# Turning the last hop's results in 32x32 blocks on VectorE instead of TensorE, with some other moves

## The chip, the cores and the metric

The kernel runs on one core of a Trainium2 chip. A core has five engines that run side by side, each with its own instruction queue: TensorE (PE, matrix products and transposes into PSUM), VectorE (DVE), ScalarE (ACT), GpSimd (POOL) and SyncE (SP). In this kernel SP's queue issues most loads, POOL's queue issues the stores and the loads of features and also computes a small power, and ScalarE's queue loads the weights. Arrays that are written out and read again lie in the chip's main memory; the working tiles lie in SBUF. The metric is the device time of one execution in microseconds (us), as the median of several runs.

## The reference

The input is a matrix of features x (2708 x 512) and a weighted, symmetrically filled adjacency adj (2708 x 2708), both in float32. Four graph layers follow one another, each as x = layernorm(x + layer(x)):

```python
def _layernorm(x, axis=-1, eps=1e-5):
    m = jnp.mean(x, axis=axis, keepdims=True)
    v = jnp.var(x, axis=axis, keepdims=True)
    return (x - m) / jnp.sqrt(v + eps)

# layer 0: mean over neighbours, with a normalised mask added to the matrix
mask = adj > 0
head = mask / max(sqrt(sum(mask * mask, -1)), 1e-12)
inc = adj + head
layer0 = (inc @ x) / sum(inc, -1)

# layer 1: attention over the graph and a plain graph product, both gated
h = x @ W_sa
scores = s_left[:, None] + s_right[None, :]          # from h and a_sa
e = where(adj != 0, exp(-leaky_relu(scores, 0.01)), 0)
x_a = (e / (sum(e, 1) + 1e-5)) @ h
x_b = adj @ (x @ W_gcnb) + b_gcnb
layer1 = sigmoid(attn_a * x_a + attn_b * x_b)        # attn_*: sigmoid gates from adj @ x and x

# layer 2: four weights, three hops
out = x @ weight[0]; p = x
for idx in range(1, 4):
    p = adj @ p
    out = out + p @ weight[idx]

# layer 3: degree-normalised product, then a dense layer
a_hat = adj + eye
dinv = rsqrt(deg)                                    # deg = max(count of adj != 0 in a row, 1)
pooled = (dinv * a_hat * dinv) @ x + x
layer3 = relu(pooled @ W + b)
```

## The kernel before

**Products.** Every product with the adjacency is done in blocks of Strassen's kind: the matrix is cut in halves (1354 rows each) and the seven products of sums of blocks are formed; in layers 2 and 3 this is done at two levels, 7 x 7 products. VectorE forms the sums of adjacency blocks (tiles called z, s, t, a), TensorE multiplies them (accumulators accu, accc, accd, acca), and VectorE and ScalarE add the results into tiles called q. Layer 2 is evaluated from the inside: the stage before the hops forms Y0 = x W3, and each of the three hops multiplies with the adjacency and adds one more term x W. Results of a sweep are transposed: features lie on partitions and nodes along the row. So a result has to be turned before it can be normed by row or be loaded as the next product's operand.

**Order of the work.** A Python function builds a list of events: `at(pos, fn)` notes that `fn` emits its instructions at position `pos`. The list is sorted by position and run, so positions are the kernel's own clock. One unit is some 12 to 13 us. The stages start at `S[s] = 28 * s`: S[0] is layer 0, S[1] and S[2] are layer 1 (S[2] ends with layer 2's first products), S[3], S[4] and S[5] are the three hops, S[6] is layer 3. A tile scheduler then orders each engine's instructions. `held` events and the early part of the list are kept in the list's order by extra dependencies without a semaphore (the loop at the end of the kernel, L1758 to 1767).

**A hop.** `sweep2` (L1351) runs over two ranges of columns, g = 0 and 1 (338 and 339 columns, times two blocks). In each range the 49 products end with two half ranges h of the nodes, and for each of these a function done(p0, dp, g, i0, n, h, cc, tiles) is called with six tiles: four of 128 nodes and two of 82 or 83. The adjacency loads of the whole sweep are issued on SP's queue, in the list's order (`load`, L1373).

**What follows a hop.** After the first two hops it is `hop_done` (L1551 to 1575): for each tile, VectorE does four block transposes (L1565; each 32x32 block is turned by itself, and the blocks are laid out by the output's access pattern) into a row buffer y, and POOL's queue stores it with four DMAs (L1570), whose rows come out in the right order in memory. After the last hop it is `done5` (L1577 to 1587): TensorE turns the tile with four transposes into a PSUM bank ps_n (`untranspose2`, L1541, instructions at L1544); `layernorm` (L598) forms the statistics on VectorE (bn_stats L600, bn_aggr L602, add L604), a power on POOL (L605), one more small operation on VectorE (L607) and the scaling on ScalarE (L610); `store2` (L1321) stores the rows to X3 on POOL's queue (L150 and L152). Row buffers come from one set of six (`nat`), used in turn.

**The next layer's operand.** `next_x2(S[6], X3)` (L308) loads X3 as the quarters B11, B12 (into T3), B21, B22 on POOL's queue, and VectorE forms their sums. `next_x(S[1], ...)` does the same for layer 1's sweep, out of X1, which layer 0 stores with POOL.

**Other places that the change touches.** `extra1` counts the nonzero entries of the adjacency in masks (tally, L1042), for the degrees, on VectorE. `prep2` (L1157) forms the attention weights e on ScalarE (L1163, L1164) and masks them on VectorE (L1165). `pairs2` (L1224) works off two half ranges of layer 1 together: it norms, turns (f), forms sums (z, L1193) and multiplies with W3 (g, L692). `ext_loads` and `ext_sums` (L1331, L1340) load blocks of layer 2's transposed input and store their sums Es for the hops. `done6` (L1639) does the dense layer, the norm and the output of layer 3.

The function done5 and its caller are the core:

Of the kernel before, what the change touches and what calls it, by code (L numbers as in the profile page):

```python
# [21 lines left out]
F32 = mybir.dt.float32  # L22
BF = mybir.dt.bfloat16
AF = mybir.ActivationFunctionType
# [3 lines left out]
NH = 1354  # L28
# [40 lines left out]
def gnn_kernel(ctx: ExitStack, tc: tile.TileContext, x, adjT, w_sa, a_sa, w_gcn, b_gcn, wab, bab, w_hop, w_out,  # L69
               b_out, out):  # L70
    nc = tc.nc
# [52 lines left out]
        return [dram.tile([wt(t % KT), D], F32, name=f"{nm}{t}", tag=f"{nm}{t}") for t in range(NT)]  # L124

    X1, XB, X2, Y0, X3 = (feature(nm) for nm in ("X1_", "XB_", "X2_", "Y0_", "X3_"))
    Y1, Y2 = ([dram.tile([NH, D], F32, name=f"{nm}{h}", tag=f"{nm}{h}") for h in range(2)] for nm in ("Y1_", "Y2_"))
    X0 = [x[h * NH + k * P : h * NH + k * P + wt(k), :] for h in range(2) for k in range(KT)]
    OUT = [out[h * NH + k * P : h * NH + k * P + wt(k), :] for h in range(2) for k in range(KT)]

# [45 lines left out]
    events = []  # L176

    held = set()

    def at(pos, fn, hold=False):  # L180

# [68 lines left out]
    def x_load(src, k, s, eng):  # L250
# [2 lines left out]
        t = b12_tile(k) if s == "B12" else new_x(s, k)  # L253
        move(eng, t[:w], q)

    def next_x(base, src, sums=0.95, halves=-0.25):


        q = nc.gpsimd

        ql = nc.scalar if base == S[1] else q
        at(base + 1.3, lambda: rest_x(src, ql))
        for k in range(KW):
            f = k / KT
            if (k * P) < RANGES[-1][0]:
                at(base - 5.8 + f, lambda k=k: x_load(src, k, "B11", q))
                at(base - 1.85 + f, lambda k=k: x_load(src, k, "B22", q))
                at(base - 1.84 + f, lambda k=k: x_load(src, k, "B12", q))
                at(base + (0.03 if base == S[1] else -1.15) + f, lambda k=k: x_sums(k), True)
                at(base - 0.85 + f, lambda k=k: x_load(src, k, "B21", q))  # L270
                at(base + 1.5 + f, lambda k=k: x_last(k), True)
            else:
                at(base + halves + 0.05 * (k - 8), lambda k=k: x_load(src, k, "B22", ql))
                at(base + max(halves, 0.1) + 0.05 * (k - 8), lambda k=k: x_load(src, k, "B21", ql))
                at(base + sums + 0.03 * (k - 8), lambda k=k: x_sums(k), True)
                at(base + 2.6 + 0.03 * (k - 8), lambda k=k: x_last(k), True)
# [31 lines left out]
    def next_x2(base, src, ext_src=None, one=False, plus=False, swapped=False):  # L308
# [7 lines left out]

        def go(s, ks, ext):
            for k in ks:
                x_load(src, k, s, q)
            if ext and ext_src is not None:  # L320
                c0 = HD if s in ("B12", "B22") else 0
                for i, g in enumerate("BD"):
                    r0 = (HD if s in ("B21", "B22") else 0) + i * P
                    h = "T3" if s == "B12" else s
                    if g == "D" and ks[-1] < 8:
                        group(h, g)
                    t, w = groups[h, g][0][:, 2, :], ext_src[r0 : r0 + P, :]
# [13 lines left out]
        if plus:  # L341
            at(base - 1.4, lambda: residual("B22"), True)
            at(base + 1.9, lambda: residual("B11"), True)
        for s, p in (("B22", 0.0 if one else -1.95), ("B21", 0.02), ("B11", late), ("B12", late + 0.15)):
            ks = list(range(KW))
            if s in early:
                lo, m = early[s]
                at(base + lo, lambda s=s, m=m: go(s, range(m), True))
                ks = range(m, KW)
            at(base + p, lambda s=s, ks=ks: go(s, ks, ks[0] == 0))  # L350
# [244 lines left out]
                     [(h * KT + k, k * P - R0, wt(k)) for k in ts])  # L595


    def layernorm(dsts, y, w, on_scalar=False, late=None):  # L598
        st = small.tile([P, 6], F32, name="st")
        nc.vector.bn_stats(st[:w], y[:w])  # L600
        mv = small.tile([P, 2], F32, name="mv")
        nc.vector.bn_aggr(mv[:w], st[:w])  # L602
        rstd = small.tile([P, 2], F32, name="rstd")
        nc.vector.tensor_scalar(rstd[:w, 0:1], mv[:w, 1:2], EPS, None, ALU.add)  # L604
        nc.gpsimd.tensor_tensor(rstd[:w, 1:2], rstd[:w, 0:1], neg_half[:w], ALU.pow)  # L605
        if on_scalar:
            nc.vector.scalar_tensor_tensor(rstd[:w, 0:1], mv[:w, 0:1], -1.0, rstd[:w, 1:2], ALU.mult, ALU.mult)  # L607
        for d, c0, c1 in dsts:
            if on_scalar:
                fn = lambda d=d, c0=c0, c1=c1: nc.scalar.activation(d[:w], y[:w, c0:c1], AF.Identity,  # L610
                                                                    bias=rstd[:w, 0:1], scale=rstd[:w, 1:2])
                fn() if late is None else late.append(fn)
                continue
            nc.vector.tensor_scalar(d[:w], y[:w, c0:c1], mv[:w, 0:1], rstd[:w, 1:2], ALU.subtract, ALU.mult)
# [416 lines left out]
    def extra1(pb, r, R0, n, A):  # L1031
# [9 lines left out]
                d = deg[R0, h]  # L1041
                nc.vector.scalar_tensor_tensor(d[:w, :n], a[:w, :n], 0.0, d[:w, :n], ALU.not_equal, ALU.add)  # L1042

        for ij, p in (("11", -0.6), ("21", 0.05), ("22", 1.05), ("12", 3.6)):
            for k in range(KW):
                at(pb + p + 0.8 * k / KT, lambda ij=ij, k=k: tally(int(ij[0]) - 1, (ij, k)), r == 0)
        for h, p in ((1, 2.0), (0, 4.5)):
# [151 lines left out]
    def pairs2(p0, R0, n, C, tiles):  # L1199
        Y = {}  # L1200
        at(p0 + 0.2, lambda: Y.update(row_sums({(i, c): C[1 - i, c] for i in range(2) for c in range(DC)}, n)))
        for i, (t0, lo, w) in enumerate(tiles):
# [45 lines left out]
            for j in range(2):  # L1248
                at(p + 0.26 * j, lambda j=j, b=b: b(j))
                at(p + 0.45 + 0.02 * j, lambda j=j, e=e: e(j))  # L1250
                at(p + 0.84 + 0.06 * j, lambda j=j, f=f: f(j), nc.tensor)
                at(p + 1.22 + 0.22 * j, lambda j=j, g=g: g(j), nc.tensor)
            at(p + 0.4, c)
            at(p + 0.92, z)

    def done2(p0, dp, last, R0, n, h, C, tiles):
        if not last:
# [288 lines left out]


    for i in range(4):
        for g, p in enumerate((S[2] + 19.3 + 1.1 * i, S[3] + 6.6 + 1.3 * i)):
            a = ({}, g, i // 2, i % 2)  # L1550
            at(p, lambda a=a: ext_loads(*a))  # L1551
            at(p + 0.5 + 0.6 * g, lambda a=a: ext_sums(*a))
# [22 lines left out]
        return done  # L1575

    def done5(p0, dp, g, i0, n, h, cc, tiles):  # L1577
        for i, (s, lo, w) in enumerate(tiles):
            r0 = i0 + s * n + lo

            def b(s=s, lo=lo, w=w, r0=r0):
                ps = untranspose2(cc, s, lo, w)
                y = nat("o")
                layernorm([(y, 0, D)], ps, w, True)
                store2(X3, y, h, r0, w)

            at(p0 + 0.1 + 0.24 * i, b)
# [51 lines left out]
    def done6(p0, dp, g, i0, n, h, cc, tiles):  # L1639

        end = (g, h) == (1, 0)
        def finish(s, lo, w, x, y):

            nc.vector.scalar_tensor_tensor(x[:w], y[:w], 0.0, x[:w], ALU.max, ALU.add)
            layernorm([(x, 0, D)], x, w, True)
            r0 = i0 + s * n + lo
            move(nc.sync, out[h * NH + r0 : h * NH + r0 + w, :], x[:w])
# [77 lines left out]
    for n, i in enumerate(list(nc.cur_bb.bb.instructions)):  # L1725
# [5 lines left out]
        if n < strict:  # L1731
            last[i.engine] = i
        done[i.engine] = i


# [35 lines left out]
```

## Time and profile before

| what | value |
|---|---|
| median of 3 runs | 2843.93 us (2843.19 to 2844.54) |
| profiled execution | 2845.44 us |
| its span | 2843.7 us |
| PE busy | 2802.4 us, 11550 instructions |
| DVE busy | 2247.7 us, 5862 instructions |
| ACT busy | 533.7 us, 1124 instructions |
| POOL busy | 617.2 us, 1114 instructions |
| HBM read and written | 425.35 MB and 83.66 MB, 179 GB/s over the span |

The span is the profiler's time from the first to the last instruction; the profiled execution's own time lies 1.74 us above it. Busy times are sums over an engine's instructions, and matrix products that overlap are counted once in an engine's share. POOL's busy time includes the issue of its DMAs; SP's DMA issues do not count as busy. In a line for a group of instructions the fields are: line, engine, operation, output and inputs, shapes, count, then busy time, mean ns of one, and the idle time of the engine just before them with what released it. In a timeline the first two numbers are start and duration in us, and brackets hold the idle time before.

### The profile page before, as it was taken

The page shows a single profiled execution, that of the slowest core. Times are in us where ns is not written, and L with a number is a line of the kernel's source. Part 1 is how long each engine was busy: PE and PEld are TensorE (multiplying, and loading weights), DVE is VectorE, ACT ScalarE, POOL GpSimd, SP SyncE. Part 2 cuts the span into 40 slices and gives each one's busy share as a digit, 9 for nine tenths or more (in the row PEclk, how much of TensorE's full clock was granted, in tenths as well). Part 3 has the DMA queues.
Part 4 walks back from the last instruction along what each step waited for, and adds up shares of the span by engine and source line. Part 5 has one row for each costly group of instructions (what it writes and reads, how often), then busy time and mean ns, then how long its engine had stood idle before and what let it go on. Part 6 is the DMA issues. An engine that isn't in the chain of part 4 may idle for free.

```text
span 2843.7 us, 38764 instructions
## 1 busy us (share of the span) xinstructions
PE 2802.4 (99%) x11550; PEld 1939.7 (68%) x11550; DVE 2247.7 (79%) x5862; ACT 533.7 (19%) x1124; POOL 617.2 (22%) x1114
## 2 busy tenths in 40 slices
PE   7999999999999999999999999999999999999998
PEld 6899765658755667866666666666666666666665
DVE  6999699668737676775699778897888878899987
ACT  4644100101155353450100000000000100100001
POOL 0223223214310011223113033030330211601202
PEclk9999999999999999999999999999999999999999
DMA  8765476446534242665678667566675666854542
GB/s 234 241 195 184 140 228 218 150 131 196 189 92 139 78 152 69 203 194 158 205 205 255 192 208 234 163 210 203 197 235 173 189 194 180 243 167 146 179 142 90
DMA packets 370291, 511.72 MB, mean 180 GB/s; under 512 B 63632, under 2 KB 323460, under 8 KB 370080
## 3 DMA queue, kind: packets, MB, share of 16 engines
q1 hardware_dynamic: 303544, 371.61, 44.1%
q0 software_dynamic: 49376, 126.39, 13.3%
q10 hardware_dynamic: 17160, 11.24, 1.4%
q8 instruction: 92, 1.51, 0.2%
q14 instruction: 119, 0.97, 0.1%
HBM read 425.35 MB, written 83.66 MB: 179 GB/s over the span
## 4 chain that ended last, share of the span: by engine, by line
PE 86%; DVE 7%; issue 2%; DMA 1%; SPq 1%; ACT 1%; POOL 1%; POOLq 0%; DVEq 0%; ACTq 0%
PE accu L1437 12%; PE accd L1437 12%; PE accc L1437 12%; PE accu L489 7%; PE accd L489 7%; PE acca L1437 6%; PE ps L692 5%; PE accc L489 5%; PE acca L489 4%; PE accr L1508 2%; PE ps_d L653 2%; PE accd L475 2%; PE accc L475 2%; PE accu L475 2%; PE acca L475 1%
## 5 line engine op out<-in xcount | busy, mean ns | idle before, releaser
L1382 DVE TENSOR_TENSOR z<-z 128x339 f32<-128x339 f32 (+1 forms) x966 | 456.8, 507 | 10.9 <-PE accu L1437 2.9
L605 POOL TENSOR_TENSOR rstd<-rstd,neg_half 128x1 f32<-128x1 f32 (+3 forms) x91 | 61.2, 674 | 770.5 <-DVE rstd L604 484.0
L1455 ACT COPY q<-accu 128x338 f32<-128x338 f32 (+1 forms) x84 | 34.6, 443 | 996.5 <-PE accu L1437 836.2
L1437 PE MATMUL accc<-s,t 128*128 128x338 f32 (+1 forms) x644 | 198.1, 450 | 0.0
L1437 PE MATMUL accd<-z,t 128*128 128x338 f32 (+1 forms) x644 | 193.9, 448 | 1.4 <-DVE q L1519 1.4
L1437 PE MATMUL accc<-z,t 128*128 128x338 f32 (+1 forms) x644 | 193.5, 448 | 0.5 <-ACT q L1455 0.5
L1437 PE MATMUL accu<-z,t 128*128 128x338 f32 (+1 forms) x644 | 193.8, 448 | 0.0
L1570 POOL DMA_DIRECT2D Y<-y x192 | 104.8, 552 | 362.8 <-DVE y L1565 331.3
L419 DVE TENSOR_TENSOR a<-a,a 128x384 f32<-128x384 f32 (+2 forms) x330 | 164.2, 514 | 6.7 <-PE accu L489 5.5
L1437 PEld LDWEIGHTS accc<-s,t 128*128 128x128 f32 x644 | 120.9, 190 | 64.1 <-issue 7.5
L1437 PEld LDWEIGHTS accc<-z,t 128*128 128x128 f32 x644 | 122.0, 190 | 61.6 <-issue 1.0
L1437 PEld LDWEIGHTS accd<-z,t 128*128 128x128 f32 x644 | 121.9, 190 | 61.1 <-DVE q L1519 2.1
L1437 PEld LDWEIGHTS accu<-z,t 128*128 128x128 f32 x644 | 121.8, 190 | 59.9 <-issue 0.5
L1382 DVE TENSOR_TENSOR s<-z 128x338 f32<-128x338 f32 (+1 forms) x322 | 150.6, 506 | 9.1 <-PE accc L1437 7.7
L1461 DVE TENSOR_TENSOR q<-q,accd 128x338 f32<-128x338 f32 (+1 forms) x112 | 56.3, 503 | 122.4 <-PE accd L1437 122.4
L1163 ACT ACTIVATE e<-row,s_right 128x384 f32<-128x384 f32 (+5 forms) x176 | 95.7, 570 | 119.8 <-PE accc L489 28.5
L1165 DVE SCALAR_TENSOR_TENSOR a<-a,e 128x384 f32<-128x384 f32 (+2 forms) x160 | 77.0, 507 | 35.7 <-ACT e L1164 25.1
L1042 DVE SCALAR_TENSOR_TENSOR masks<-a,masks 128x384 bf16<-128x384 f32 (+2 forms) x152 | 76.0, 507 | 12.3 <-DMA a<-in_adjT 11.3
L422 POOL DMA_DIRECT2D As<-a x120 | 64.7, 542 | 88.3 <-DVE a L419 64.0
L829 DVE SCALAR_TENSOR_TENSOR s<-a,row 128x384 f32<-128x384 f32 (+2 forms) x152 | 75.8, 511 | 7.5 <-ACT row L814 7.5
L825 DVE TENSOR_TENSOR run<-run,a 128x384 f32<-128x384 f32 (+2 forms) x156 | 77.9, 499 | 1.4
L1164 ACT ACTIVATE e<-e 128x384 f32<-128x384 f32 (+5 forms) x176 | 78.7, 477 | 1.4
(787 smaller groups left out, 5957.6 us busy)
## 6 DMA issues: line engine op xcount, KB each, us to landing
z<-As SPq DMA_DIRECT2D x320, 169.5 KB
z<-As SPq DMA_DIRECT2D x320, 169.0 KB
a<-in_adjT SPq DMA_DIRECT2D x240, 192.0 KB
z<-in_adjT SPq DMA_DIRECT2D x240, 169.5 KB
z<-in_adjT SPq DMA_DIRECT2D x240, 169.0 KB
a<-in_adjT SPq DMA_DIRECT2D x120, 165.0 KB
a<-in_adjT SPq DMA_DIRECT2D x112, 128.0 KB
As<-a POOLq DMA_DIRECT2D x60, 192.0 KB, 3.5
```

The source lines that it names most:

```text
L419: nc.vector.tensor_tensor(A[r, dst, k][:, :n], A[r, a, k][:, :n], A[r, b, k][:, :n], op)
L475: nc.tensor.matmul(B[home, c][:, c0 : c0 + w], a[:, i * P : (i + 1) * P], x[:, d : d + w], start=bool(start and c0 == 0), stop=stop, skip_ ...
L489: nc.tensor.matmul(B[home, c][:, :n], X[STAT[p], k][:, c * P : (c + 1) * P], A[r, MOV[p], k][:, :n], start=bool(start and k == k0), stop=k ...
L692: nc.tensor.matmul(H[home][:w], Y[a, c][:, lo : lo + w], wop(v, c), start=part == 0 and home in "ud" and c == 0, stop=c == 1, skip_group_c ...
L825: nc.vector.tensor_tensor(run[R0, h][:w, :n], run[R0, h][:w, :n], t[:w, :n], ALU.add)
L1042: nc.vector.scalar_tensor_tensor(d[:w, :n], a[:w, :n], 0.0, d[:w, :n], ALU.not_equal, ALU.add)
L1163: nc.scalar.activation(e[:w, :n], row[R0, h][:w, :n], AF.Prelu, bias=s_right[:w, t : t + 1], alpha=0.01)
L1164: nc.scalar.activation(e[:w, :n], e[:w, :n], AF.Exp, scale=-1.0)
L1165: nc.vector.scalar_tensor_tensor(a[:w, :n], a[:w, :n], 0.0, e[:w, :n], ALU.not_equal, ALU.mult)
L1382: nc.vector.tensor_tensor(d[:, :n], Z[x + (k,)][:, :n], Z[y + (k,)][:, :n], op)
L1437: nc.tensor.matmul(B[home][:, :n], stat(v, k), a[:, :n], start=bool(start and k == 0), stop=k == nk - 1, skip_group_check=True)
L1570: nc.gpsimd.dma_start(out=rows[:, :, f * P : (f + 1) * P], in_=o[32 * f : 32 * (f + 1), : m * P].rearrange("p (b d) -> p b d", d=P))
```

## The change

The last hop's results are turned as those of the first two hops are, except in the half range (g, h) = (1, 0), which is the last. For the other three half ranges VectorE turns blocks, POOL stores the tile to a new array Y3, SP's queue fetches it as rows, and the layernorm works on that tile. The rows come with their blocks in a different order along the row, so ScalarE's scaling writes with a permuted access pattern (`swapped`). X3 is stored as before.

Several positions in the list move too: some loads of features get a dependency without a semaphore on the last power emitted before them (`behind_power`, `powers`, `ties`), which orders them behind it on POOL; layer 1's late B11 loads come 0.5 units later, and layer 3's B22 loads 0.65 later; the first range's count masks of block 11 come 0.75 later; in pairs2 the turning, the sums and the products come 0.04 to 0.07 later; the sums Es for the first range of the hops come 1.2 to 2.25 units earlier; and the first half range of layer 3 is worked off 0.35 units later.

```diff
-    Y1, Y2 = (...)
+    Y1, Y2, Y3 = (...)
+    powers, ties = [], []
+    def behind_power(fn):
+        n = len(nc.cur_bb.bb.instructions)
+        fn()
+        if powers:
+            ties.extend((i, powers[-1]) for i in range(n, len(nc.cur_bb.bb.instructions)))
...
-                at(base - 5.8 + f, lambda k=k: x_load(src, k, "B11", q))
-                at(base - 1.85 + f, lambda k=k: x_load(src, k, "B22", q))
-                at(base - 1.84 + f, lambda k=k: x_load(src, k, "B12", q))
+                for s, p in (("B11", 5.8 - 0.5 * (base == S[1] and k > 2)), ("B22", 1.85), ("B12", 1.84)):
+                    at(base - p + f, lambda k=k, s=s: behind_power(lambda: x_load(src, k, s, q)))
...
-                x_load(src, k, s, q)
+                behind_power(lambda: x_load(src, k, s, q)) if base == S[6] else x_load(src, k, s, q)
...
-        for s, p in (("B22", 0.0 if one else -1.95), ("B21", 0.02), ("B11", late), ("B12", late + 0.15)):
+        for s, p in (("B22", 0.0 if one else -1.3 if base == S[6] else -1.95), ("B21", 0.02), ("B11", late), ("B12", late + 0.15)):
...
-    def layernorm(dsts, y, w, on_scalar=False, late=None):
+    def swapped(t):
+        return t.rearrange("p (c f d) -> p f c d", c=4, d=32)
+    def layernorm(dsts, y, w, on_scalar=False, late=None, swap=False):
...
+        powers.append(len(nc.cur_bb.bb.instructions) - 1)
...
+                o, i = d[:w], y[:w, c0:c1]
+                if swap:
+                    o, i = swapped(o), i.rearrange("p (f c d) -> p f c d", c=4, d=32)
+                fn = lambda o=o, i=i: nc.scalar.activation(o, i, AF.Identity, bias=rstd[:w, 0:1], scale=rstd[:w, 1:2])
...
-        for ij, p in (("11", -0.6), ("21", 0.05), ("22", 1.05), ("12", 3.6)):
+        for ij, p in (("11", -0.6 if r else 0.15), ("21", 0.05), ("22", 1.05), ("12", 3.6)):
...
-                at(p + 0.84 + 0.06 * j, lambda j=j, f=f: f(j), nc.tensor)
-                at(p + 1.22 + 0.22 * j, lambda j=j, g=g: g(j), nc.tensor)
+                at(p + 0.9 + 0.06 * j, lambda j=j, f=f: f(j), nc.tensor)
+                at(p + 1.26 + 0.22 * j, lambda j=j, g=g: g(j), nc.tensor)
-            at(p + 0.92, z)
+            at(p + 0.99, z)
...
-        for g, p in enumerate((S[2] + 19.3 + 1.1 * i, S[3] + 6.6 + 1.3 * i)):
+        for g, p in enumerate((S[2] + 18.1 + 0.75 * i, S[3] + 6.6 + 1.3 * i)):
...
     def done5(p0, dp, g, i0, n, h, cc, tiles):
+        if (g, h) != (1, 0):
+            hop_done(Y3)(p0, 0.24, g, i0, n, h, cc, tiles)
+            for i, (s, lo, w) in enumerate(tiles):
+                got = {}
+                r0 = i0 + s * n + lo
+                def a(w=w, r0=r0, got=got):
+                    got["y"] = y = nat("ld")
+                    move(nc.sync, y[:w], Y3[h][r0 : r0 + w, :])
+                def b(w=w, r0=r0, got=got):
+                    o = nat("o")
+                    layernorm([(o, 0, D)], got["y"], w, True, swap=True)
+                    store2(X3, o, h, r0, w)
+                at(p0 + 0.75 + 0.24 * i, a)
+                at(p0 + 1.05 + 0.24 * i, b)
+            return
...
     def done6(p0, dp, g, i0, n, h, cc, tiles):
+        if (g, h) == (0, 0):
+            p0 += 0.35
...
+    instructions = list(nc.cur_bb.bb.instructions)
+    for i, j in ties:
+        tc.add_manual_dep(instructions[i], instructions[j].name,
+                          mybir.DependencyInfo(mybir.DependencyClass.NoSync, mybir.DependencyReason.DATA),
+                          reason="order of the list")
```

More of the change, by code (lines that the diff above doesn't have):

```diff
@@ L126, in gnn_kernel @@
     X1, XB, X2, Y0, X3 = (feature(nm) for nm in ("X1_", "XB_", "X2_", "Y0_", "X3_"))
-    Y1, Y2 = ([dram.tile([NH, D], F32, name=f"{nm}{h}", tag=f"{nm}{h}") for h in range(2)] for nm in ("Y1_", "Y2_"))
+    Y1, Y2, Y3 = ([dram.tile([NH, D], F32, name=f"{nm}{h}", tag=f"{nm}{h}") for h in range(2)] for nm in ("Y1_", "Y2_", "Y3_"))
     X0 = [x[h * NH + k * P : h * NH + k * P + wt(k), :] for h in range(2) for k in range(KT)]
@@ L609, in layernorm @@
             if on_scalar:
-                fn = lambda d=d, c0=c0, c1=c1: nc.scalar.activation(d[:w], y[:w, c0:c1], AF.Identity,
-                                                                    bias=rstd[:w, 0:1], scale=rstd[:w, 1:2])
+                o, i = d[:w], y[:w, c0:c1]
+                if swap:
+                    o, i = swapped(o), i.rearrange("p (f c d) -> p f c d", c=4, d=32)
+                fn = lambda o=o, i=i: nc.scalar.activation(o, i, AF.Identity, bias=rstd[:w, 0:1], scale=rstd[:w, 1:2])
                 fn() if late is None else late.append(fn)
```

## The prediction

> **What bounds the kernel.** I read the busy shares first, then TensorE's share slice by slice, its waits, the windows in which the changed work lies, and the chain of waits at two places.
>
> ```profile
> PE 2802.4 (99%) x11550; PEld 1939.7 (68%) x11550; DVE 2247.7 (79%) x5862; ACT 533.7 (19%) x1124; POOL 617.2 (22%) x1114
> ...
> PE   7999999999999999999999999999999999999998
> ...
> DVE  6999699668737676775699778897888878899987
> ```
>
> TensorE is busy 2802.4 of 2843.7 us; the granted clock is 1.00 in every window below. So an instruction taken off TensorE is time won, unless another engine comes too late with the next operand. VectorE is second, at 79%, but above 90% in single stretches. TensorE's waits, longest sums (which tile waits for which, total, times, longest):
>
> ```profile
> PE ps L692 <- DVE d L1193: 4.4, 3, 3.4
> PE accd L489 <- DVE a L419: 3.3, 3, 1.5
> PE accd L1437 <- DVE q L1519: 1.4, 1, 1.4
> ```
>
> Behind the first 100 us these and a few shorter ones are all the idle time there is, some 15 us. Windows of 50 us, the first in the hop before, the others in the last hop (PE, PEld, DVE, ACT, POOL busy, then clock, DMA):
>
> ```profile
> 1850.00:1900.00 50.00, 50.00 (x182) 33.00 (x181) 45.92 (x112) 1.67 (x4) 9.64 (x18) 1.00 0.66 197
> 2200.00:2250.00 50.00, 50.00 (x201) 32.94 (x200) 46.81 (x117) 6.31 (x10) 13.07 (x22) 1.00 0.61 181
> 2250.00:2300.00 50.00, 50.00 (x192) 33.86 (x191) 39.95 (x102) 6.31 (x10) 15.35 (x27) 1.00 0.67 203
> 2400.00:2450.00 50.00, 50.00 (x194) 33.45 (x193) 35.65 (x93) 4.66 (x6) 25.80 (x46) 1.00 0.83 245
> ```
>
> In the last three lie the 18 tiles whose transposes move (six each near 2211-2231, 2265-2281, 2397-2417). TensorE never rests there.
>
> **The sum** is made against the profiled execution: 2845.44 us (span 2843.7), 1.51 above the median of 2843.93.
>
> *1. TensorE transposes, -7.9.* Each tile has four, between products:
>
> ```profile
> 2211.07 0.60 PE L1544 MATMUL ps_n<-ident,q 128*128 128x128 f32 x4
> 2211.50 0.73 PE L1437 MATMUL accu<-z,T3B 128*128 128x338 f32 x2
> ```
>
> From the start of the four to the start of the next product is 0.43 us; over all 24 tiles it adds up to 10.49, 0.437 each. 18 tiles: 7.9 us. The other end is the group's busy time, 14.4 us for 96, so 10.8 for 72; busy times overlap their neighbours', so I take the former. These lie on the path, since the windows are full. The Trainium skill ("VectorE: DVE Perf Modes", Rules for kernel authors) speaks against the move: for 128x128 it says to use TensorE where the result may lie in PSUM, and gives 390 ns on TensorE against 311 on VectorE (for blocks of 32 only, and in bf16). By its figure the 72 would return an estimated 28 us; the trace's own 0.437 for four decides.
>
> *2. VectorE in the last hop, +1 (0 to +6).* The same block transposes already run behind the earlier hops:
>
> ```profile
> L1565 DVE STREAM_TRANSPOSE y<-q 128x128 f32<-128x128 f32 x128 | 30.2, 286 | 0.1
> L1565 DVE STREAM_TRANSPOSE y<-q 128x96 f32<-128x96 f32 x64 | 12.4, 246 | 0.0
> ```
>
> 12 tiles x 4 x 0.286 + 6 x 4 x 0.246 = 19.6 us, 6.5 for each half range. The statistics cost the same (0.69 from PSUM or SBUF). In the first window 46.8 + 6.5 is 3.3 over 50; but the norms (some 1 us a tile) move about 12 us later, and TensorE runs 4 to 5.5 us behind VectorE there, with a least gap of 2.0. The other windows have 10 and 14 us free. The window of the hop before, with transposes of this kind, stands at 45.9 of 50 and TensorE does not wait. So 0 to 3.3 for the first, with 1 taken, and up to 6 if a second half range is caught too. ScalarE's norm with a permuted output is in no row; from SBUF a norm takes 0.81 and ScalarE is busy 6 of 50, so even doubled it only delays the store.
>
> *3. Round trip through memory, 0 (0 to +8).* POOL gets 72 more stores at 0.552 each, 40 us, all beside other work at 13 to 26 busy of 50. They land in 3.7 us. SP gets 24 fetches of 0.33 to 0.45. A fetch waits for its tile's store and for a buffer (a tile now takes three of the six shared row buffers, not one); I work out that it comes 7 to 10 us after the transposes, against 1.1 + 2.2 + 3.7 = 7.0 for transposes, four issues and landing. So it may hold SP for 4 to 6 us, and the adjacency loads behind it; those are issued 20 to 30 us before TensorE uses them and 10 to 16 before VectorE does, so they are covered. X3 then comes later, and the first loads of the next layer behind it:
>
> ```profile
> 2424.39 0.51 POOL L152 DMA_DIRECT2D X<-o  x1
> 2424.89 1.64 POOL L150 DMA_DIRECT2D B22C<-X  x3
> 2426.53 0.54 POOL L150 DMA_DIRECT2D B22D<-X  x1
> 2427.38 0.54 POOL L150 DMA_DIRECT2D B22D<-X  x1 [0.32 <-DVE z L1382]
> ```
>
> VectorE needs that B22 at 2450.2 (difference t), TensorE 1 us later. I put the last X3 store at 2430 and the last B22 at 2437, 12 us early. If all my spare is an error, the first product waits as much as X3 is later still: 8 taken as the end.
>
> *4. POOL's order at the end of layer 0, -3.3 (-3.3 to 0).*
>
> ```profile
> 345.84 0.54 POOL L150 DMA_DIRECT2D B11B<-X  x1 [4.54 <-DMA X<-o]
> 346.39 0.56 POOL L605 TENSOR_TENSOR rstd<-rstd,neg_half 128x1 f32<-128x1 f32 x1
> ```
>
> A load of B11 stands on POOL's queue ahead of the power and waits 4.54 us for the X store to land (the chain has that store for 5.67 from 339.65). VectorE waits for that power until 346.99, its sums come late, and TensorE waits 0.69, 1.10 and 1.48 at 348 to 357: 3.27. The ties put these loads behind all the powers listed before them, so the chain is cut. What is next late: the loads of T3B and T3C (B12), which move from 347-355 to about 400, and ten count masks of 0.5 that move to about 430, with VectorE at 47.9 and 46.4 of 50 and TensorE less than 1 us behind it. Price 0 to +3, 0.5 taken.
>
> *5. Layer 1 to 2, -4 (-7.2 to +2).* TensorE rests 7.2 us between 971 and 1257, 3.36 of it at 1234 before a product on sums of VectorE:
>
> ```profile
> 1222.94 0.22 issue
> 1223.16 0.01 POOLq L1345
> 1223.17 5.70 DMA Es<-s
> 1228.87 0.02 issue
> 1228.89 0.58 ACT e L1163
> 1229.47 0.02 issue
> 1229.49 0.49 ACT e L1164
> ```
>
> ScalarE's e waits for a ring buffer that an Es store holds, issued behind other POOL work. The Es sums move from 1176-1254 to about 1170-1192, so this wait goes (3.36), and POOL is lighter at 1256 (0.85). Turning and products 0.04 to 0.07 units later (0.5 to 0.9 us) give or take under 1. Against it: more ring buffers and 4 sums at a time at 1160-1190, where VectorE has 37.8 of 50: up to +2. -4 is the two waits.
>
> *6. First range of layer 3 later by 0.35 units (some 4.5 us), -1 (-2.7 to +2).* TensorE waits 1.35, 0.80 and 0.54 there (2574 to 2598); some goes, some is only moved.
>
> Sum: -7.9 + 1 + 0 - 3.3 + 0.5 - 4 - 1 = -14.7. 2845.4 - 14.7 = 2830.7; less 1.5, 2829.2 for a median, rounded to 2830.
>
> **Rivals.**
> - *Only the transposes count.* Waits 4 to 6 are replaced by others as long (VectorE is thin in all three places). -7.9 + 1 = -6.9: 2837 (2834 to 2841). For it: a wait removed often uncovers the next. Against: 4 and 5 each have one named releaser, a DMA landing, that leaves the chain.
> - *VectorE becomes the bound in the last hop.* The three windows do not absorb the 19.6 us; each half range stalls by its own 3.3, 10 in all, and part of 4 and 5 fails (4): -14.7 - 1 + 10 + 4 = -1.7, so 2842, no change. For: 46.81 of 50. Against: 39.95 and 35.65 in the others.
> - *Slower: SP is held.* A fetch that waits on SP beyond 10 us starves VectorE's z, and TensorE with it; the fetch needs POOL's stores, which stand behind powers and X3 stores of earlier tiles, so tiles can hold each other up. It is slower than before when the 18 fetches exceed the cover by over 14.7 us together, 0.8 each; at 1.5 each it is +27 - 14.7 = +12, 2856. For: all six row buffers in turn, and a queue that issues loads in 8 of the 20 us from 2225. Against: POOL is busy 26 to 50% there, and SP's own work has gaps of 3 to 5 us between groups of loads.
> - *The change does not do what it says:* TensorE would not gain if it waited after each transpose anyhow. The full windows exclude it.
>
> **The numbers.** Chances: my forecast 0.58 (own range 2821 to 2836), only the transposes 0.22, VectorE bound 0.10, SP held 0.10. The measurement tells 0.2% (5.7 us) from no change: the bounds are 2838.2 and 2849.6. Faster: all of the first, 0.20 of the second: 0.78. Same: the rest of the second and the third, with 0.02 of the fourth: 0.14. Slower: 0.08. The low end takes the best bounds, though not all together: -10.8 - 3.3 - 7.2 - 2.7 = -24 gives 2820; I take 2821. The high end, 2843, takes in the second rival and the third, and leaves out the fourth.
>
> **What would show it.** Right: 24 transposes on line 1544's successor, not 96; TensorE's busy time down by about 10.8; 264 block transposes on VectorE; TensorE still at 50 of 50 in the three windows, which come some 6 to 8 us earlier; no waits at 348-357 and at 1234. Wrong: new TensorE waits on z or s of line 1382's successor behind SP (the third rival or the second: VectorE idle for a DMA in the one, at 50 of 50 in the other); a wait for t at the start of layer 3 (step 3); TensorE's waits at 400-450 for T1 or for a (step 4); or the sum of idle time as before, though the named waits are gone.

## The result and the profile after

The changed kernel takes 2851.72 us (median of 9 runs, 2850.40 to 2853.32), the kernel before 2843.77 beside it (9 runs): a ratio of 1.0028 with a 95% interval of 1.0019 to 1.0037. It is slower by 8 us where 14 less were forecast. The profiled execution took 2852.80 us with a span of 2851.0, 7.36 more than the span before.

The shares of the page, changed kernel:

```profile
PE 2797.6 (98%) x11478; PEld 1932.3 (68%) x11478; DVE 2258.7 (79%) x5934; ACT 532.2 (19%) x1122; POOL 660.2 (23%) x1186
```

72 transposes are gone from TensorE, 72 block transposes came to VectorE and 72 stores to POOL. TensorE's busy time fell by 4.8 us (from 2802.4), and not by the 10.8 named as a sign. The windows of the last hop (PE, PEld, DVE, ACT, POOL busy, clock, DMA):

```profile
2200.00:2250.00 50.00, 47.42 (x171) 29.99 (x170) 43.95 (x117) 5.62 (x9) 21.24 (x38) 0.97 0.72 224
2250.00:2300.00 50.00, 49.11 (x171) 31.87 (x169) 43.71 (x125) 5.74 (x9) 26.24 (x46) 1.00 0.74 221
2400.00:2450.00 50.00, 50.00 (x186) 32.25 (x185) 40.41 (x116) 4.89 (x6) 35.55 (x66) 1.00 0.89 278
```

TensorE now rests in the first two, and the clock granted in the first is 0.97. VectorE, where I had feared 53 of 50, is at 43.95: it has time left, and yet TensorE waits for it. TensorE's waits behind the first 100 us, longest sums:

```profile
PE ps L706 <- DVE ld L715: 4.9, 3, 3.3
PE accu L496 <- DVE B11D L628: 3.3, 1, 3.3
PE ps_t L656 <- DVE ld L628: 2.5, 2, 1.7
PE accd L1451 <- DVE z L1396: 2.1, 4, 1.0
PE accu L1451 <- DVE z L1396: 1.9, 2, 1.1
PE accc L1451 <- DVE s L1396: 1.6, 1, 1.6
```

The waits of layer 0's end and of 1234 that stood in the list before are gone (accd for a has 0.8 left, ps for d 0.8), and others stand in their place.

**Where the time went.** I match the same products in the two traces, in order, and subtract their start times. The difference is flat where nothing happens and steps where a kernel gains or loses, so it says which stretch paid. For the changed kernel against before, one profiled execution each (us of the kernel before; stretches left out are flat):

| stretch | step | what it is |
|---|---|---|
| 0 to 330 | -1.0 | not the change: it is there by 90 us, before any edit acts, and other kernels here stand between -2.4 and +1.0 |
| 330 to 365 | -3.0 | end of layer 0 |
| 365 to 470 | +6.6 | a wait of 3.26 near 428, and half the clock behind it |
| 470 to 1300 | -0.8 | layers 1 and 2 |
| 2200 to 2430 | +1.4 | last hop: -7.9 for the transposes, +9.2 for waits and half clock |
| 2480 to 2830 | -1.6 | layer 3 |
| 2830 to the end | +5.9 | work ends 1.5 later, the span 7.4 later |

Three losses of 6 to 9 us, then, against three gains that came nearly as forecast (transposes, end of layer 0, layer 3) and one, in layers 1 and 2, that hardly came.

*The last hop.* VectorE's waits from 2200 to 2320, changed kernel:

```profile
DVE rstd L619 <- POOL rstd L616: 6.1, 10, 1.7
DVE st L611 <- DMA ld<-Y: 5.1, 5, 1.7
```

and in the kernel before:

```profile
DVE rstd L607 <- POOL rstd L605: 5.0, 8, 0.9
DVE st L600 <- PE ps_n L1544: 1.5, 2, 1.1
```

So the wait for the power is hardly new; the wait for the fetched rows (ld) is. The chain of waits that leads to TensorE's first wait there (start, us, what):

```profile
2230.09 5.70 DMA ld<-Y
2235.80 0.03 issue
2235.82 0.02 DVEq L611
2235.84 0.04 issue
2235.89 0.69 DVE st L611
...
2238.16 0.71 POOL rstd L616
2238.87 0.02 issue
2238.89 0.16 DVE rstd L619
2239.05 0.84 DVE s L1396 x2
```

The row fetch takes 5.70 us from SP's issue to landing, and it is issued late: SP stands 28.3 us in 13 waits from 2200 to 2320 until a tile's stores to Y3 have landed, 7.9 at most. The norm's statistics (st) are already next on VectorE, and the adjacency sums s stand behind them in its queue. Then the small operation behind the power waits again. TensorE's waits that follow:

```profile
2245.16 0.84 PE L1451 MATMUL accc<-s,t 128*128 128x338 f32 x2 [1.56 <-DVE s L1396]
2247.02 5.63 PE L1451 MATMUL accd<-z,t 128*128 128x338 f32 x12 [1.02 <-DVE z L1396]
2256.00 1.40 PE L1451 MATMUL accu<-z,t 128*128 128x338 f32 x4 [0.79 <-DVE z L1396]
```

*Near 428.* POOL, then VectorE and TensorE in the changed kernel:

```profile
418.41 1.64 POOL L150 DMA_DIRECT2D B21C<-X  x3
420.03 0.55 POOL L429 DMA_DIRECT2D As<-a  x1
420.60 0.58 POOL L616 TENSOR_TENSOR rstd<-rstd,neg_half 128x1 f32<-128x1 f32 x1
```

```profile
421.21 0.41 DVE L628 TENSOR_SCALAR B11D<-ld,mv,rstd 128x256 f32<-128x256 f32 x1 [3.04 <-POOL rstd L616]
```

```profile
428.22 2.93 PE L496 MATMUL accu<-a,B11D 128*128 128x384 f32 x4 [3.26 <-DVE B11D L628]
```

A norm's power stands on POOL behind loads and stores that POOL now issues at 391 to 420; VectorE waits 3.04 for it, and the next tile's norm ends at 428. In the kernel before the same power came later, but it was POOL that waited, for VectorE:

```profile
424.30 0.56 POOL L605 TENSOR_TENSOR rstd<-rstd,neg_half 128x1 f32<-128x1 f32 x1 [1.35 <-DVE rstd L604]
```

In the changed kernel four products then take 2.93 us, and the clock granted in 428 to 435 is 0.54:

```profile
420.00:428.00 8.00, 4.96 (x16) 2.62 (x14) 6.64 (x18) 0.00 (x0) 2.84 (x6) 0.97 0.89 278
428.00:435.00 7.00, 6.78 (x12) 3.79 (x13) 6.53 (x18) 0.96 (x2) 2.96 (x5) 0.54 0.34 101
```

So the wait of 3.26 cost 6.6: 3.3 more by half the clock, which the trace's clock records have for 6.83 us from 427.6.

*The end.* The last result leaves ScalarE 1.5 us later than before, but the span ends 7.4 later. What lies between is POOL's last DRAIN instruction, which the views do not count as busy; from the trace's own records (start, us):

```
before    DRAIN 2838.89  3.69    span 2843.66   POOL DMAs 1016
changed   DRAIN 2840.42  9.81    span 2851.01   POOL DMAs 1088
```

### The profile page after: what moved, and what is told of

It reads as the page before. It is cut to its first block, busy times and chain, and to the rows that moved or that the text cites. A ratio compares the mean times of both kernels' runs of the same rounds, so it can differ in the third digit from the quotient of the medians.

```text
span 2851.0 us, 38824 instructions
## 1 busy us (share of the span) xinstructions
PE 2797.6 (98%) x11478; PEld 1932.3 (68%) x11478; DVE 2258.7 (79%) x5934; ACT 532.2 (19%) x1122; POOL 660.2 (23%) x1186
## 4 chain that ended last, share of the span: by engine, by line
PE 83%; DVE 7%; DMA 3%; issue 2%; POOL 2%; ACT 1%; SPq 1%; POOLq 0%; ACTq 0%; DVEq 0%
PE accc L1451 12%; PE accu L1451 12%; PE accd L1451 12%; PE accd L496 6%; PE accu L496 6%; PE accc L496 6%; PE acca L1451 6%; PE ps L706 5%; PE acca L496 3%; PE accr L1522 3%; PE ps_d L667 2%; PE accd L482 2%; PE accc L482 2%; PE accu L482 1%; POOL rstd L616 1%
## 5 line engine op out<-in xcount | busy, mean ns | idle before, releaser
L1584 POOL DMA_DIRECT2D Y<-y x264 | 144.6, 554 | 561.6 <-DVE y L1579 525.4
```

What stands on the lines that cost most here:

```text
L1584: nc.gpsimd.dma_start(out=rows[:, :, f * P : (f + 1) * P], in_=o[32 * f : 32 * (f + 1), : m * P].rearrange("p (b d) -> p b d", d=P))
```

## The experiments

My theory A after reading the trace: three separate costs. The rivals are named with each run. All times are compared with runs of the kernel before on the same chip, whose median was between 2843.3 and 2847.1 from one set of runs to the next. The table has the steps of each kernel's profiled execution against the one of the kernel before, in the stretches above; the text after it gives the time. A step holds what differs between two executions as well: from 470 to 1300 it is -0.4, 3.3 and 2.6 in y3_only, pool72 and pool24, which change nothing there.

| kernel | to 330 | 330-365 | 365-470 | 470-1300 | 1300-2200 | 2200-2430 | 2430-2480 | 2480-2830 | to the end |
|---|---|---|---|---|---|---|---|---|---|
| changed | -1.0 | -3.0 | 6.6 | -0.8 | 0.0 | 1.4 | 0.0 | -1.6 | 5.9 |
| y3_only | 0.1 | 0.6 | 0.0 | -0.4 | 0.0 | 4.5 | 6.4 | 0.0 | 5.8 |
| moves_only | 0.3 | -2.3 | 5.2 | 1.3 | 0.0 | 0.0 | 0.0 | -1.6 | 0.2 |
| stores_act | 0.7 | -2.7 | 4.5 | 3.2 | 0.0 | 3.8 | 0.0 | -1.6 | 0.0 |
| masks_early | 1.0 | -2.4 | 4.0 | 2.4 | 0.0 | 2.5 | 0.0 | -1.6 | 5.8 |
| norm_late | 0.5 | -3.1 | 4.3 | 2.4 | 0.8 | -6.6 | 0.0 | -1.7 | 5.8 |
| ties_b11 | -0.5 | -1.6 | 1.5 | 4.0 | 0.9 | 2.0 | 0.0 | -1.6 | 5.9 |
| pool72 | -0.2 | -0.3 | 0.0 | 3.3 | 0.6 | 0.0 | 0.0 | 0.0 | 6.5 |
| pool24 | 0.0 | 0.2 | 0.0 | 2.6 | 0.7 | 0.0 | 0.0 | 0.1 | 1.4 |
| fixed | -0.9 | -2.2 | 1.5 | 0.3 | 0.2 | -7.3 | 0.0 | -1.7 | 5.8 |
| fixed_x3act | -2.4 | -3.1 | 1.5 | -0.8 | 0.0 | -6.5 | 6.8 | -1.7 | 2.2 |
| fixed_x3act_ext | 0.3 | -3.0 | 1.5 | 0.0 | 0.0 | -7.3 | 7.5 | -1.7 | 2.2 |
| plain_store | -1.6 | -2.5 | 1.5 | 0.4 | 0.0 | -8.1 | 4.2 | -1.7 | -0.3 |
| best | -2.1 | -1.7 | 1.5 | 1.8 | 0.0 | -7.9 | 2.6 | -1.4 | -0.1 |
| best_masks | -0.4 | -2.1 | 0.0 | 0.9 | 0.0 | -8.1 | 3.3 | -1.4 | -0.1 |

### The two halves of the change

y3_only puts the new done5 and its norm into the kernel before, and one position:

```diff
-        for s, p in (("B22", 0.0 if one else -1.95), ...
+        for s, p in (("B22", 0.0 if one else -1.3 if base == S[6] else -1.95), ...
```

> The kernel before with the new path of the last hop alone (block transposes, Y3, row fetch, permuted norm; the next layer's B22 loads 0.65 units later, since X3 is written later in the list). Theory A (three separate costs: a stall at 428 us from the moves, VectorE held by its own row fetches in the last hop, and POOL's final drain, which grows with POOL's number of DMAs): no stall near 428; the last hop gives 7.9 us for the transposes and loses about 9 to waits; POOL's last drain is 9.8 us and not 3.7; in all +7 against before, about 2851. Theory B (the drain grows from the moves, not from the 72 stores): drain 3.7, about +1.4, 2845.

Measured: 2864.90 us against 2846.75, ratio 1.0066 (1.0052 to 1.0080). Nothing near 428, and the last drain is 9.81, as theory A has it. But it is 18 us slower and not 7: 3 more in the last hop, and 6.4 at 2430 to 2480, where the changed kernel loses nothing. The chain there:

```profile
2442.81 0.54 POOL B22D L150
2443.36 0.57 POOL rstd L609
2443.94 0.02 issue
2443.96 0.15 DVE rstd L611
2444.12 0.43 DVE z L1388
2444.55 0.04 issue
2444.59 1.91 PE accu L1443 x4
```

A load of the next layer's B22 stands ahead of a power on POOL, VectorE waits for the power, and TensorE for VectorE's z: the same line-up as at the end of layer 0 before. In the changed kernel the last of these powers (2435.63) runs ahead of all loads of B22 (from 2436.30); the ties of layer 3's loads, which y3_only does not have, order it so. So they seem to belong to the new path; no run takes them alone away.

moves_only takes the new path out and keeps the rest:

```diff
-        if (g, h) != (1, 0):
+        if False:
             hop_done(Y3)(p0, 0.24, g, i0, n, h, cc, tiles)
```

> The changed kernel with the old done5, so all moves and no Y3. Theory A: -1 at the start, -3.0 at the end of layer 0, +6.6 near 428 (a wait of 3.3 and half the clock for 6.8 us), -0.8 in layers 1 and 2, -1.6 in layer 3, drain 3.7: about the time before, 2844. Theory B: the drain of 9.8 comes with it, 2850.

Measured: 2849.50 against 2846.75, 1.0008 (0.9999 to 1.0017). The drain is 3.69. The moves win 2.3 and 1.6 and lose 5.2 near 428: as theory A has it, nothing is left of them. Theory B falls.

### POOL's last drain

```diff
+                    for f in range(3 if dst is Y1 else 0):      # 1 in pool24
+                        nc.gpsimd.dma_start(out=spare[:, :, f * P : (f + 1) * P], in_=(the same part of o))
```

> The kernel before with 72 more DMAs on POOL's queue in the first hop (copies of three quarters of each result tile, which nobody reads). If the last drain follows from the number of POOL's DMAs alone: 9.8 us in place of 3.7, and the span 6 longer. If it follows from Y3's stores in the last hop or their neighbours, 3.7.

> The kernel before with 24 such DMAs. If the drain grows in proportion to the number of added DMAs (0.085 us each): 3.7 + 2.0 = 5.7. If it goes in a step, 3.7 or 9.8.

Of these two there is one profiled execution each. The 72 stores stand in the first hop, 900 us before the end, and the last drain is 10.22 us; with 24 it is 5.40. The work itself is untouched from 1300 on (steps of 0.6 and 0.7 at most, and none behind 2200). So the drain grows with POOL's number of DMAs, wherever they stand: 0.07 and 0.09 us for each that was added. Together with the later runs:

```
POOL DMAs    983   1002   1016   1037   1040   1088
last DRAIN  1.89   3.44   3.69   6.14   5.40   9.81 (10.22 in pool72)
```

The bytes don't set it: POOL's queue moves 126.56 MB in the kernels with 1037 DMAs (6.14) and with 983 (1.89) alike. But the order at 1037 and 1040 is the wrong way round, so the number is not all of it. Up to about 1016 the drain is over before SP has seen the last store land, and costs nothing; before, it was just at that edge.

stores_act moves the 72 stores off POOL:

```diff
-            hop_done(Y3)(p0, 0.24, ...)
+            hop_done(Y3, nc.scalar)(p0, 0.24, ...)      # the four stores on ScalarE's queue
```

> The changed kernel with the 72 stores to Y3 on ScalarE's queue in place of POOL's. Theory A: POOL issues as many DMAs as before, so its last drain is 3.7 again, -6.1; VectorE's waits for the power in the last hop (6.1 in all) get shorter too, as no stores stand ahead of it, for 0 to -3: 2843 to 2846. Theory B: drain stays at 9.8, 2849 to 2852.

Measured: 2853.52 against 2846.75, 1.0022 (1.0014 to 1.0031). The drain is 3.69 and the end costs nothing, as expected; but the last hop takes 3.8 in place of 1.4 and layers 1 and 2 take 3.2 (a wait of 3.31 at 1215 stands in the changed kernel too, but here half the clock follows it for 6.83 us), so the time hardly moves. VectorE's waits for the rows (2200 to 2330, then 2390 to 2470) in this kernel are longer than in the changed one:

```profile
DVE st L611 <- DMA ld<-Y: 7.7, 6, 2.2
DVE rstd L619 <- POOL rstd L616: 4.2, 8, 0.8
```

```profile
DVE st L611 <- DMA ld<-Y: 6.6, 3, 3.4
```

Relief on POOL shortened the waits for the power by 2 and did not help: the row is what comes late. SP's queue suffers as well: from 2200 to 2330 its adjacency loads wait 16.9 us for stores to Y3 to land, where there was no such wait in the changed kernel.

### The wait near 428

```diff
-        for ij, p in (("11", -0.6 if r else 0.15), ...
+        for ij, p in (("11", -0.6), ...
```

> The changed kernel with the count masks of block 11 in layer 1's first range back at their old place in the list. If the masks' move makes the norm at 421 to 428 wait for POOL (nothing is then left on VectorE to cover the power, which stands behind B21's loads), the stall near 428 and the half clock go: -6.6, 2845. If the ties or the later B11 loads make it, the stall stays: 2852.

Measured: 2856.02 against 2846.75, 1.0032 (1.0020 to 1.0045). The wait at 428 is gone, but one of 1.81 comes at 419, for a result that VectorE adds (P1c), with 3.41 us of half clock behind it; the stretch still loses 4.0. So it is not the masks' move that loses the time here.

```diff
-  behind_power(lambda: x_load(src, k, s, q)))
+  behind_power(lambda: x_load(src, k, s, q)) if s == "B11" else x_load(src, k, s, q))
```

> The changed kernel with the new order behind the powers kept for layer 1's B11 loads only, not for its B22 and B12 loads (layer 3's ties stay). Theory A (the T3B and T3C loads that move from 347-355 to 395-405 crowd POOL and VectorE there, and the norms' chain through POOL ends too late for the product at 425): the gain of 3.0 at 350 stays, the wait of 3.3 and the half clock near 428 go, -6 against the changed kernel, +2 against before. Rival D (the product at 425 was as late as its norm allowed before already, so 3 us gained ahead of it turn into a wait in any case): the wait near 428 stays within 1 us, and the time is that of the changed kernel, +8 against before.

Measured: 2854.04 against 2846.79, 1.0023 (1.0014 to 1.0032). TensorE has no wait at 395 to 445 and the clock stays; 5 of the 6.6 are won back, though the gain at 330 to 365 is 1.6 here and not 3.0. VectorE's wait of 3.04 for the power is 0.05. The ties on the B22 and B12 loads were the cause; of these loads, those that changed place are T3B's and T3C's (395 to 405 in the changed kernel, 354 to 357 here). Rival D falls too, most clearly in later kernels with this mend: in plain_store and fixed_x3act TensorE comes to this place 4.1 and 5.5 us earlier than before, in the changed kernel 4.0, and it does not wait. What stays is 1.5 near 450, a wait for the masks (below). The time as a whole did not show it: +7 and not +2. Of that, 4.0 came between 470 and 1300, where the two POOL runs beside it, which change nothing there, show 3.3 and 2.6 too; so this stretch differs from one set of runs to the next by more than this edit weighs.

### The last hop

```diff
-                at(p0 + 0.75 + 0.24 * i, a)
-                at(p0 + 1.05 + 0.24 * i, b)
+                at(p0 + (1.4 if g == 0 else 0.75) + 0.24 * i, a)
+                at(p0 + (2.2 if g == 0 else 1.05) + 0.24 * i, b)
```

> The changed kernel with the row fetch of the first range's twelve tiles 0.65 units (8 us) later and their norm 1.15 units (15 us) later. Theory A (VectorE starts a norm's statistics before the row has landed, waits 5 us for rows and 6 for powers in 2200 to 2320, and the adjacency sums behind it come late): the TensorE waits of 2245 to 2307 go and the transposes' full 7.9 us are won there, so -9 against the changed kernel, -1 against before. Rival C (VectorE simply has too much work, 6.5 us more per half range): the waits stay at 6 to 9, only at other places, and the time is that of the changed kernel, +8 against before. POOL's last drain stays at 9.8 in both.

Measured: 2848.67 against 2846.79, 1.0007 (0.9998 to 1.0016). The last hop wins 6.6 in place of losing 1.4. Its windows and VectorE's waits (2200 to 2330):

```profile
2200.00:2250.00 50.00, 50.00 (x187) 32.58 (x186) 46.13 (x113) 3.14 (x7) 14.80 (x27) 1.00 0.72 224
2250.00:2300.00 50.00, 49.63 (x174) 32.65 (x173) 47.48 (x140) 7.26 (x11) 29.75 (x50) 1.00 0.80 244
```

```profile
DVE rstd L619 <- POOL rstd L616: 6.4, 9, 3.1
DVE q L1475 <- PE accd L1451: 2.9, 1, 2.9
DVE q L1475 <- PE accc L1451: 0.5, 2, 0.3
```

The wait for ld is gone, the waits for the power are as long as in the changed kernel, and TensorE rests 0.4. SP still stands 24.9 us, in 14 waits, for the stores to Y3, so it was not SP's standing that cost the time. VectorE does the same work (46 and 47 of 50), only in an order in which it never stands before a row that is still on its way. Rival C, too much work, falls.

### Both mends, and what stood behind them

fixed has the edits of norm_late and ties_b11 together.

> The changed kernel with both mends: the first range's row fetch and norm later in the last hop, and layer 1's ties on B11 alone. Theory A: the two gains add, -6 for the last hop and -1 to -6 near 428; the last drain stays at 9.8: between -4 and 0 against before. If one mend spoils the other (both use POOL, but 1800 us apart), it stays at +2.

Measured: 2841.01 against 2843.32, 0.9994 (0.9985 to 1.0003); the profiled spans differ by 4.2. The gains add. The work ends 10.05 us earlier, and the drain of 9.81 takes 5.8 of it back.

fixed_x3act then stores X3 from ScalarE's queue (18 tiles), and fixed_x3act_ext puts the sums Es back too:

```diff
-                    store2(X3, o, h, r0, w)
+                    store2(X3, o, h, r0, w, nc.scalar)
```

```diff
-        for g, p in enumerate((S[2] + 18.1 + 0.75 * i, S[3] + 6.6 + 1.3 * i)):
+        for g, p in enumerate((S[2] + 19.3 + 1.1 * i, S[3] + 6.6 + 1.3 * i)):
```

> The same with the stores to X3 on ScalarE's queue, behind the norm's scaling that ScalarE does itself: 1037 DMAs on POOL, not 1088. If the drain goes with the number of DMAs (3.7 at 1016, 5.4 at 1040, 9.8 at 1088): 5.2, so -4.6 against the kernel without this. If it goes with the bytes or descriptors stored since some earlier point, it may differ. In the last hop nothing new waits (ScalarE is busy 12% there).

> The same again with the sums Es for the hops' first range back at their old, later place. If their move is what gives the new waits of 3.3 and 1.7 near 1214 and 1228 (VectorE's and the loads' work comes together there), 1075 to 1300 gets 2 to 4 shorter. If the move cures the old wait of 3.4 at 1234 and the new ones have another cause, 1075 to 1300 gets 3 to 7 longer (the old wait and its half clock).

Measured: 2842.83 and 2844.66 against 2843.32, 0.9996 (0.9987 to 1.0005) and 1.0001 (0.9992 to 1.0010). The drain is 6.14 in both, a little more than I reckoned. More than it gives goes at the start of layer 3: a wait of 3.1 there (4.0 in fixed_x3act_ext) with 6.83 us of half clock, 6.8 in all (7.5). My "nothing new waits" was wrong. The chain ahead of that wait holds a landing store of X3 (4.05 us) and then two adjacency loads of SP (4.67 and 8.06): from 2385 to 2445 SP's adjacency loads wait 9.0 us for X3's stores, and not at all in fixed. That is the rival "SP is held", in a place where the prediction did not look for it.

Between 470 and 1300 the two differ by 0.8. With the sums at their old place the old wait is back, with its chain through a landing Es store:

```profile
1236.29 3.29 PE L706 MATMUL ps<-w,d 128*128 128x256 f32 x8 [3.49 <-DVE d L1207]
```

```profile
1221.99 6.08 DMA Es<-s
```

and the waits of 3.3 and 1.7 near 1210 and 1225 are gone. With the sums early, as in fixed, it is the other way round, and again a landing Es store stands ahead of ScalarE's e, 35 us sooner:

```profile
1188.42 5.63 DMA Es<-a
1194.06 0.02 issue
1194.08 1.03 ACT e L1177 x2
```

The move takes the wait at 1234 away, and hands it to another product. Both of my two expectations came true at once, and the sum is near nothing.

plain_store starts from fixed_x3act. It stores a tile to Y3 as it lies, by one DMA, and lets SP's fetch do the ordering:

```diff
-            hop_done(Y3)(p0, 0.24, g, i0, n, h, cc, tiles)
...
+                    nc.gpsimd.dma_start(out=box[:, : m * P], in_=o[:, : m * P])
...
-                    move(nc.sync, y[:w], Y3[h][r0 : r0 + w, :])
+                    rows = box.rearrange("(f i) (b d) -> b i f d", i=32, d=P)
+                    for b in range(m):
+                        u, v = max(off, 32 * b), 32 * (b + 1)
+                        nc.sync.dma_start(out=y[u - off : v - off, :].rearrange("p (f d) -> p f d", d=P),
+                                          in_=rows[b, u - 32 * b : 32, :, :])
```

> The kernel with both mends and X3's stores on ScalarE, and Y3 stored as it lies in the tile, by one DMA a tile on POOL in place of four; the order of the rows is then made by the fetch, three or four DMAs a tile on SP in place of one or two. 983 DMAs on POOL: drain 3.7 or less, so -1.5 or more against the kernel before this step. SP gets 42 more issues of 0.35 to 0.4, 15 us, beside other work: nothing, if adjacency loads stay ahead; up to 5 if they don't.

Measured: 2838.32 against 2843.32, 0.9983 (0.9975 to 0.9992). The drain is 1.89 and no longer counts; the full transposes' gain comes, 8.1; 4.2 are lost at the start of layer 3.

best leaves X3's stores of the half range (1, 1) on POOL, and best_masks puts the masks back as well:

```diff
+                    store2(X3, o, h, r0, w, nc.scalar if g == 0 else None)
...
-        for ij, p in (("11", -0.6 if r else 0.15), ...                # best_masks alone
+        for ij, p in (("11", -0.6), ...
```

> Y3 stored by one DMA a tile and fetched in blocks, both mends, and X3 stored from ScalarE's queue in the first range only; the half range (1, 1), whose X3 the next layer wants at once, stores from POOL. If the three terms found (the last hop's waits for rows and powers, the wait near 428, the last drain) are all that was missing in the sum, TensorE's work ends about 10 us earlier than before, as in the kernel with the two mends, and the drain (about 1005 DMAs, 3.7 or less) adds nothing: -9 to -11 against before, 2833. If something else is still hidden, for instance a cost of the first product of layer 3 whoever stores X3 (a wait of 3.1 and the half clock at 2442), it stays at -5, as in the kernel with all X3 stores on ScalarE.

> The same with the count masks of block 11 back at their old place. With the loads no longer crowding POOL there, the wait of 1.25 for the masks near 448 (their last use) goes, and nothing comes near 428: -1.5 against the kernel without this. If the masks at their old place hold VectorE before the norms at 405 to 425, as in the run with the masks alone put back, a wait of 2 to 5 comes there, and it is slower by that.

Measured: best 2839.33 and best_masks 2837.79 against 2847.09; 0.9974 (0.9964 to 0.9985) and 0.9965 (0.9952 to 0.9977). Both are faster than the kernel before, by 0.3%, and than the changed one (1.0028 against the kernel before). best stays a little short of -9: 2.6 are still lost at 2430 to 2480. The waits view shows 0.4 of it. Most of the rest lies in the starts of products from 2424 to 2431 that read z, up to 1.24 us apart where 0.285 is the rule in this trace: VectorE makes these z between the last norms of the half range (1, 1), which neither mend moves (both positions change for g = 0 alone), and waits 6.7 us for their powers from 2400 to 2431, 0.9 in fixed. Why these powers come later was not settled. With the masks at their old place the 1.5 near 450 go, as expected.

## Why the prediction was wrong

1. *Transposes, -7.9: right.* The difference between the traces drops by 0.44 at each of the 18 tiles, by 7.86 in all, and with the waits gone a kernel keeps most or all of it (-6.5 to -8.1).
2. *VectorE in the last hop, +1 (0 to +6): this failed, +9.2.* I added up busy time and left out what VectorE stands before. The step "the statistics cost the same" is true of their duration; but they now wait for a fetch that lands 5.7 us after its issue, 0.3 units (4 us) behind it in the list, and everything behind them on VectorE waits too (5.1 us in this stretch, with TensorE's waits of 1.56, 1.02 and 0.79 and half the clock behind). The rival "VectorE becomes the bound" came near in size (10), with the wrong mechanism: VectorE was busy 43.95 of 50, and norm_late, which moves fetch and norm later, cures it with the same work. That near hit is luck.
3. *Round trip, 0 (0 to +8): right about SP and the start of layer 3, wrong about POOL.* SP does stand before fetches (none of its issues falls between 2206.1 and 2215.8), and no adjacency sum of VectorE waited for a load from 2200 to 2320. The last store of X3 came at 2439.6 and not at 2430, the last load of B22 at 2444.7 and not at 2437 (TensorE's work is 3.1 us later there), still soon enough. The step "72 more stores, 40 us, all beside other work" left out that POOL's last drain grows with them: +5.9 at the end.
4. *End of layer 0, -3.3: right (-3.0). The price behind it, 0 to +3 with 0.5 taken: this failed, +6.6.* The place was named (the T3B and T3C loads that move to about 400), but not that a norm's power stands behind them on POOL, nor that the wait would bring half the clock.
5. *Layers 1 and 2, -4: this failed, -0.8.* The wait at 1234 went as worked out, and with it 6.83 us of half clock that the prediction had not counted. Waits of 3.3 and 1.7 came 10 to 25 us earlier; that the wait would be handed on was not in the sum. The size -0.8 is that of one execution. But in all eleven kernels with the early sums the difference falls by some 8 us from 1228 to 1262 and rises by 5.8 to 9.9 from 1200 to 1228, so the trade itself is sure.
6. *Layer 3, -1: right in sign, -1.6* (and there in every kernel that has the edit).

The sum of what I had priced wrongly is 8.2 (last hop) + 5.9 (drain) + 6.1 (428) + 3.2 (layers 1 and 2), 23.4; smaller terms take it to the 22 by which the forecast missed. The rival that ended slower, SP held, was not what happened: no wait of SP before a fetch passed 8 us, and norm_late keeps these waits and wins. Its sign, VectorE idle for a DMA, was there, but the DMA was the row fetch itself and not an adjacency load.

## What to carry to other kernels

When work moves from the bounding engine to one with time to spare, don't add up busy time alone: ask of each moved instruction what it waits for, and what is queued behind it. A step that reads back what was just stored belongs so late in the list that the landing time shown in the trace (here 3.3 to 5.7 us for each way) is over. And look at the end of the program too: what a queue has to clear up there can eat the gain.

## What the runs showed of the hardware

- POOL's last DRAIN grew from 1.9 to about 10 us between 983 and 1088 DMAs on its queue, and extra DMAs 900 us before the end count as well.
- Half the clock followed some waits of TensorE and not others, and for 3.41 or 6.83 us in the records. Behind the wait of 3.26 at 428 it was 6.83 us (3.3 lost), behind a cluster of 1.56 and 1.02 within 2 us at 2245 it was 3.41, and behind 1.81 at 419 in masks_early 3.41; but 2.5 at 428 in norm_late brought none. The same wait of 3.31 near 1210 brought none in the changed kernel and in moves_only, 3.41 in fixed and plain_store, and 6.83 in stores_act and ties_b11. The Trainium skill ("TensorE: Matmul & The Clock Gate", Part 1) speaks of windows of 3413 ns that run free of the kernel; the lengths agree with one and two of these. That the gate falls after an idle window does not cover the cluster, in which TensorE worked between the waits. The kernel before had such a stretch too, 6.83 us from 1233.5 behind its wait of 3.36; the prediction gives the clock only for windows without one.
